# One delta-rule decoder layer: GpSimd in the order of emission, six buffers for queries and P, four for A^, two for x, block-join copies on ScalarE

## The chip, the cores and the metric

The kernel runs as one launch on one core of one Trainium2 chip. A core has five engines that each work through a queue of their own: TensorE (PE) for matmuls and transposes, VectorE (DVE), ScalarE (ACT), GpSimd (POOL), and SyncE (SP), which here only issues DMAs. [...] The metric is device microseconds (us) of one execution; lower is better.

## The reference

A decoder layer on x of shape (4, 512, 512), float32 throughout, with three residual parts. The change lies in the first, a gated delta rule with 16 heads of 128:

```python
x = x + attn(layernorm(x))        # delta rule, below
x = x + cross_attn(layernorm(x), ctx)   # 16 heads of 32, quantised
x = ffn(layernorm(x))             # causal attention with RoPE, then 8 experts, 2 per token; both residuals inside

# attn, per batch and head
q, k, v = (silu(causal_conv4(x @ W.T)) for W in (Wq, Wk, Wv))
g = exp(-exp(A_log) * softplus(x @ Wa.T + dt_bias)); beta = sigmoid(x @ Wb.T)
q, k = q / norm(q), k / norm(k)
for t in range(512):              # the state S is 128 x 128
    error = v[t] - g[t] * (S.T @ k[t])
    S = g[t] * S + outer(k[t], beta[t] * error)
    o[t] = S.T @ q[t]
o = o * rsqrt(mean(o * o) + 1e-6) * norm_w * silu(x @ Wg.T)
return o @ Wo.T
```

## The kernel before, in words

The recurrence is done in chunks of 128 tokens. Inside a chunk, the effect of the tokens on each other is a triangular system whose matrix (called A^ here, tile `at`) is inverted; between chunks a 128x128 state is carried. The work is cut into 32 *pairs* m = 0 to 31: 4 batches times 8 pairs of heads (HG = 2). A pair goes through these generators:

- `stage1(m)`: keys. Projection and convolution (`conv`, whose matmuls are L503, and its three DVE products L514), transposes with sums of squares `ss` (L551, L557), five small GpSimd operations on [128, 8] tiles L558 to L562 (`rk` is a power, `ee` and `ke` scales, `nr` norms), the decay matrix `em` (a scan on DVE L567, then scaled on ACT L397 by `ee`), `at` (L579) which goes to DRAM and comes back as 32x32 blocks `iA` (L633). Then queries: `qg` (query times decay, GpSimd L590), P = keys times queries times decay (`pt`, DVE L601), and the query norm `rq`, which goes through a DMA from `sr` (L614) and two GpSimd operations (L622, L623).
- `stage2_inverse(m)`: elimination of the 32x32 diagonal blocks in 31 steps of two operations, L644 and L645 (`iW`, `iT`), on DVE for even m and on GpSimd for odd m; then a transposed copy (L649) on the same engine. The results go to DRAM (L648, L650) and come back as the 128x128 tiles `T` (L653) and `X` (L655).
- `stage2_values(m)`: values `vn` and gates `gs`.
- `stage3(m)`: the *join* of the inverted blocks into a 128x128 inverse, by small matmuls (L704 and L705, L714 and L716, L727, L736) with copies out of PSUM in between (`Y`, L707 and L708; `T` and `X`, L718 to L720), then the chain over four chunks (L758, L760, L767, L769, L777, L782) with output products L785 and L787, and a tail: `og` (L796), `cv` (L800), its square on ACT (L804), added into `acc` on GpSimd (L805). `rb` is the row of query norms (L742); the gate product `gs * rb` is L745 on GpSimd.
- `output(m)`: output projection (L825), summed in `xa`; after the last pair of a batch, the norm and the residual.
- `prologue(b)`: layernorm, transposes and gates of the next batch, with x loaded at L406. `prepare()` computes keys and values of the cross attention ahead of the loop.

The main loop takes stage3 of pair m, and between its steps it advances, by `turns`, output of m-1 by one step, stage1 of m+2 by two, values of m+1 by one and the inverse of m+1 by two:

```python
            rest = turns(*rest)
            for _ in stage3(m):
                next(rest, None)
            run(rest)
```

`stage3` yields 15 times, so 30 of the 31 elimination steps are emitted inside this loop, and the 31st after stage3's tail. The emission order is only a priority: a planner reorders each engine's queue by its own estimate of when inputs are ready. On TensorE it keeps almost to the emission; on DVE and GpSimd it moves much. [...] Tiles are in pools: a tile named with bufs=4 has four places, and the fifth waits until the first one's readers are done. After the 32 pairs come cross attention, causal attention and experts, which the change doesn't touch.

Of the kernel before, what the change touches and what calls it, by code (L numbers as in the profile page):

```python
# [98 lines left out]
def decoder(ctx: ExitStack, tc: tile.TileContext, a: dict, out: bass.AP):  # L99
# [69 lines left out]
    def idle(n):  # L169
        for _ in range(n):  # L170
            yield
# [154 lines left out]
    with ExitStack() as st:  # L326
# [74 lines left out]
        def prologue(b):  # L401

            x = []
            for c in range(TB):
                t = w2.tile([P, D], F32, name="x_in", bufs=4)
                nc.sync.dma_start(t, x_t[:, b * TB + c, :])  # L406
                x.append(t)
            yield
            yield
            for c, t in enumerate(x):  # L410
                run(layernorm(t.unsqueeze(1), t.unsqueeze(1), small))
                if c == 0:
                    xnT = s2.tile([P, KD, S], F32, name="xnT", bufs=2)
                    seqs[b] = [xnT]
                tp = p_b.tile([P, KD, P], F32, name="pb")
                for kd in range(KD):
                    nc.tensor.transpose(tp[:, kd, :], t[:, kd * P : (kd + 1) * P], ident)
                nc.scalar.copy(xnT[:, :, c * P : (c + 1) * P], tp)
                yield
            pab = p_b.tile([P, TB, 32], F32, name="pb")  # L420
            for c in range(TB):
                for kd in range(KD):
                    nc.tensor.matmul(pab[:, c, :], xnT[:, kd, c * P : (c + 1) * P], wab[:, kd, :], start=kd == 0, stop=kd == KD - 1)
            g_a, lg, beta, gam, ngam, gend, gall = (seq.tile([P, H1, TB], F32, name=n) for n in ("g_a", "lg", "beta", "gam", "ngam", "gend", "gall"))
            nc.scalar.activation(beta, pab[:, :, 16:32].rearrange("p i h -> p h i"), AF.Sigmoid)
            nc.vector.tensor_tensor(g_a, pab[:, :, 0:16].rearrange("p i h -> p h i"), along(dtb, TB), ALU.add)


            y, z, w = (small.tile([P, H1, TB], F32, name=n, bufs=1) for n in ("sp_y", "sp_z", "sp_w"))
            nc.vector.scalar_tensor_tensor(y, g_a, -1.0, g_a, ALU.mult, ALU.min)  # L430
            nc.scalar.activation(y, y, AF.Exp)
            yield
            nc.vector.tensor_scalar(w, y, 2.0, None, ALU.add)
            nc.vector.reciprocal(w, w)
            nc.vector.tensor_tensor(z, y, w, ALU.mult)
            nc.vector.tensor_tensor(w, z, z, ALU.mult)
            nc.vector.tensor_scalar(y, w, 1.0 / 17, None, ALU.mult)
            for n in (15, 13, 11, 9, 7, 5, 3):
                nc.vector.scalar_tensor_tensor(y, y, 1.0 / n, w, ALU.add, ALU.mult)
                if n in (11, 5):  # L440
                    yield
            nc.vector.scalar_tensor_tensor(y, y, 1.0, z, ALU.add, ALU.mult)
            nc.vector.tensor_scalar(y, y, 2.0, None, ALU.mult)
            nc.vector.scalar_tensor_tensor(y, g_a, 0.0, y, ALU.max, ALU.add)
            nc.vector.scalar_tensor_tensor(y, y, -1.0, along(alog, TB), ALU.mult, ALU.mult)

            nc.vector.tensor_scalar(lg, y, -200.0, None, ALU.max)
            yield

            lgf = lg.rearrange("p h i -> p (h i)")  # L450
            pg = p_b.tile([P, 3, H1 * TB], F32, name="pb")
            for n, m in enumerate((C_UP, C_LO, C_ONE)):
                nc.tensor.matmul(pg[:, n, :], tab_a[:, m, :], lgf, start=True, stop=True)
            for n, dst in enumerate((gam, gend, gall)):
                nc.scalar.activation(dst.rearrange("p h i -> p (h i)"), pg[:, n, :], AF.Exp)
            nc.vector.tensor_scalar(ngam, gam, -1.0, None, ALU.mult)
            yield

            nc.vector.tensor_scalar(y, lg, -87.0, None, ALU.max)
            nc.vector.tensor_scalar(z, y, float(np.log2(np.e)), None, ALU.mult)  # L460
            nc.vector.tensor_scalar(z, z, MAGIC, MAGIC, ALU.add, ALU.subtract)
            nc.vector.scalar_tensor_tensor(y, z, -0.693145751953125, y, ALU.mult, ALU.add)
            nc.vector.scalar_tensor_tensor(y, z, -1.42860677e-06, y, ALU.mult, ALU.add)
            yield
            nc.vector.tensor_scalar(w, y, 1.0 / 5040, None, ALU.mult)
            for n in (720, 120, 24, 6, 2, 1):
                nc.vector.scalar_tensor_tensor(w, w, 1.0 / n, y, ALU.add, ALU.mult)
            n2 = small.tile([P, H1, TB], mybir.dt.int32, name="n2", bufs=1)
            nc.vector.tensor_scalar(n2, z, 127.0, None, ALU.add)
            nc.vector.tensor_scalar(n2, n2, 23, None, ALU.logical_shift_left)  # L470
            nc.vector.scalar_tensor_tensor(w, w, 1.0, n2.bitcast(F32), ALU.add, ALU.mult)
            yield

            tp = p_b.tile([H1 * TB, 2, P], F32, name="pb")
            nc.tensor.transpose(tp[:, 0, :], w.rearrange("p h i -> p (h i)"), ident)
            nc.tensor.transpose(tp[:, 1, :], gam.rearrange("p h i -> p (h i)"), ident)
            gr = w2.tile([P, TB * 64], F32, name="Y6").rearrange("p (n t) -> p n t", n=2)[0 : H1 * TB]
            nc.scalar.copy(gr, tp)
            nc.gpsimd.memset(gr[:, 0, 0:1], 0.0)
            for n in range(2):  # L480
                nc.sync.dma_start(g_d[b, n], gr[:, n, :])
            seqs[b] += [beta, gam, ngam, gend, gall]
            yield
# [38 lines left out]
        def stage1(m):  # L522
# [48 lines left out]
            for p in range(HG):  # L571
                scale(em[p], em[p], ee, p)
                pk = p_b.tile([P, TB, P], F32, name="pb")
                for c in range(TB):
                    k_ = kT[p][:, c * P : (c + 1) * P]
                    nc.tensor.matmul(pk[:, c, :], k_, k_, start=True, stop=True)
                at = live.tile([P, TB, P], F32, name="at", bufs=6)
                ats.append(at)
                nc.vector.scalar_tensor_tensor(at, pk, -1.0, em[p], ALU.mult, ALU.mult)  # L579
                nc.sync.dma_start(squares(at_d[m % SLOTS][p * TB : (p + 1) * TB]), at)  # L580
# [5 lines left out]
            for p in range(HG):  # L586
                q = s1.tile([P, S], F32, name="qh")
                yield from conv(b, hg, p, 0, wq, q)
                g = live.tile([P, S], F32, name="qg", bufs=4)
                nc.gpsimd.tensor_tensor(g, q, mb[p], ALU.mult)  # L590
                qg.append(g)
                t = w2.tile([P, S], F32, name="cv", bufs=5)
# [4 lines left out]
                for c in range(TB):  # L597
                    cs = slice(c * P, (c + 1) * P)
                    nc.tensor.matmul(pq[:, c, :], kT[p][:, cs], q[:, cs], start=True, stop=True)
                t = live.tile([P, TB, P], F32, name="pt", bufs=4)  # L600
                nc.vector.tensor_tensor(t, pq, em[p], ALU.mult)  # L601
                pt.append(t)
                yield
# [86 lines left out]
        def stage3(m):  # L690
# [13 lines left out]
                    nc.tensor.matmul(py[lo[p], c, :], ats[p][:, c, 32:64], Ts[p][:, c, 0:32], start=True, stop=True)  # L704
                    nc.tensor.matmul(py[hi[p], c, :], ats[p][:, c, 96:128], Ts[p][:, c, 64:96], start=True, stop=True)  # L705
            for p in range(HG):
                nc.vector.tensor_copy(Yd[p][32:64, :, 0:32], py[lo[p]])  # L707
                nc.scalar.copy(Yd[p][96:128, :, 32:64], py[hi[p]])  # L708
            yield
            px = p_b.tile([P, TB, 96], F32, name="pb")  # L710
# [4 lines left out]
                for p in range(HG):  # L715
                    nc.tensor.matmul(px[half[p], c, 0:64], Yd[p][:, c, :], odd(Xs[p][:, c, :]), start=True, stop=True)  # L716
            for p in range(HG):
                nc.vector.tensor_copy(Ts[p][32:64, :, 0:32], px[lo[p], :, 64:96])  # L718
                nc.scalar.copy(Xs[p][0:32, :, 32:64], px[lo[p], :, 0:32])
                nc.vector.tensor_copy(Xs[p][64:96, :, 96:128], px[hi[p], :, 32:64])  # L720
            yield

            Y6 = []
# [17 lines left out]
            t = w2.tile([P, HG, S], F32, name="rrow", bufs=1)  # L741
            nc.sync.dma_start(chunks(t), r_d[m % SLOTS].rearrange("c t -> (c t)").partition_broadcast(P))  # L742
            rb = [t[:, p, :] for p in range(HG)]
            for p in range(HG):
                nc.gpsimd.tensor_tensor(gs[p], gs[p], rb[p], ALU.mult)  # L745

            st_ = [None] * HG
            po = [p_o.tile([P, TB, P], F32, name=f"po{p}") for p in range(HG)]
            for c in range(TB):
# [34 lines left out]
                for p in range(HG):  # L784
                    nc.tensor.matmul(po[p][:, c, :], us[p], pt[p][:, c, :], start=True, stop=c == 0)  # L785
                    if c > 0:
                        nc.tensor.matmul(po[p][:, c, :], st_[p], qg[p][:, cs], start=False, stop=True)  # L787
                st_ = nst
                yield

            og = []
# [18 lines left out]
        def output(m):  # L810
# [4 lines left out]
            wot = w2.tile([P, HG, D], F32, name="wot", bufs=2)  # L815
            nc.sync.dma_start(wot, a["a_wo"][hg])
            xs = []
            if hg == NHG - 1:
                for c in range(TB):
                    xs.append(w2.tile([P, D], F32, name="x_in", bufs=4))  # L820
                    nc.sync.dma_start(xs[c], x_t[:, b * TB + c, :])
            for c in range(TB):
                pw = p_b.tile([P, D], F32, name="pb")
                for p in range(HG):
# [7 lines left out]
            if hg == NHG - 1:  # L832
# [6 lines left out]
                rsqrt(rs, pq, small, add=1e-6, mul=1.0 / VD)  # L839
                yield  # L840
                for c in range(TB):
                    xr = xs[c]
                    nc.vector.scalar_tensor_tensor(xr, xa[c], rs[:, c : c + 1], xr, ALU.mult, ALU.add)

                    (nc.gpsimd if m == NP - 1 else nc.sync).dma_start(x1d[b * TB + c], xr)
                    yield

        def prepare():

            ctx_ = [w2.tile([P, D], F32, name="og", bufs=2) for _ in range(2)]  # L850
            for kt in range(2):
                nc.sync.dma_start(ctx_[kt], a["ctx"][kt * P : (kt + 1) * P])
            wk = [w2.tile([P, D], F32, name="x_in", bufs=4) for _ in range(KD)]
            for kd in range(KD):
                nc.sync.dma_start(wk[kd], a["b_wkv"][kd * P : (kd + 1) * P, 0:D])
            wv = [w2.tile([P, HG, D], F32, name="wot", bufs=2) for _ in range(2)]
# [31 lines left out]
            for c in range(KD):  # L888
# [14 lines left out]
                yield  # L903
                nc.sync.dma_start(x_val_d[:, :, c * P : (c + 1) * P], t.rearrange("p (k c) -> p k c", k=2))

        NP = B * NHG
        load_weights(0, 1, 0, 2, 3, by=nc.scalar)
        start = prologue(0)
# [11 lines left out]
        for m in range(NP):  # L920
# [13 lines left out]
                wx = top.enter_context(tc.tile_pool(name="b_x", bufs=2, side="right", reuse_waits="tile"))  # L934
                rest.append((cross(0), 2))
            if m:
                rest.append((output(m - 1), 1))
            if m + 2 < NP:
                if (m + 2) % NHG == 0:
                    assert (m + 2) // NHG in seqs  # L940
# [574 lines left out]
```

## Time and profile before

The median of three runs is 3922.55 us (3909.57 to 3927.0). The profiled execution took 3921.34 us, its span is 3919.6 us.

| What | us |
|---|---|
| span of the profiled execution | 3919.6 |
| start of the join of pair 0 (first L704) | 148.5 |
| start of the join of pair 31 | 2113.1 |
| PE busy over the span | 3487.2 |
| DVE busy | 2238.4 |
| ACT busy | 1522.5 |
| POOL busy | 1373.3 |
| PE busy between 148.5 and 2113.1 (1964.6 long) | 1766.48 |
| DVE busy there | 1270.76 |
| ACT busy there | 787.81 |
| POOL busy there | 924.44 |
| mean granted TensorE clock, whole span | 0.941 of full |

Times are those of one execution, read by the hardware profiler. "Busy" leaves out instructions that only wait, branch or issue a DMA. A wait is written as *waiting instruction <- what released it*, with the total, the count and the longest. A line number is a line of the kernel before. "T0" below is the start of the first join matmul (L704) of a pair, and "T0+30" is 30 us later.

### The profile page before, as it was taken

To read this page: it belongs to the slowest core of one execution; us is meant where nothing else is said; L and a number is where in the kernel's file an instruction comes from. 1 tells how busy PE (TensorE), PEld (TensorE's weight loads), DVE (VectorE), ACT (ScalarE), POOL (GpSimd) and SP (SyncE) were. 2 spreads that over 40 slices of the span, in tenths; PEclk is the share of its full clock that TensorE was granted. 3 is DMA by queue.
4 is the path that set the end of the run, shared out by engine and by line. 5 is a ranking of instruction groups with operands and counts; after the bars stand their busy time and mean duration, and the time that the engine had idled before them with its cause. 6 is when DMAs were issued, how large, how long until landed. Compare 5 with 4: busy or idle time off the path is not lost. (4 is left out here: it accounts for less than half of the span.)

```text
span 3919.6 us, 48951 instructions
## 1 busy us (share of the span) xinstructions
PE 3487.2 (89%) x16466; PEld 1984.1 (51%) x16466; DVE 2238.4 (57%) x5115; ACT 1522.5 (39%) x4190; POOL 1373.3 (35%) x1941
## 2 busy tenths in 40 slices
PE   5898899898989989898989799998998999897897
PEld 3455555555555555555555445554554555453343
DVE  5576657675766666756765466555665655543111
ACT  3434443334343434334333244443443444433121
POOL 1443554344435552455335222112212211210442
PEclk8899999899999998999999899998999999898898
DMA  5324332433243333343332444445444444445344
GB/s 163 107 77 123 98 103 80 130 101 111 82 119 119 98 100 106 97 119 104 96 98 87 158 145 154 137 132 132 146 127 137 153 146 139 141 152 183 79 82 93
DMA packets 391881, 465.56 MB, mean 119 GB/s; under 512 B 128451, under 2 KB 242115, under 8 KB 391440
## 3 DMA queue, kind: packets, MB, share of 16 engines
q1 hardware_dynamic: 380080, 438.03, 37.1%
q0 software_dynamic: 10112, 21.58, 3.1%
q8 instruction: 132, 2.16, 0.2%
q10 hardware_dynamic: 1440, 2.84, 0.2%
q14 instruction: 117, 0.96, 0.1%
HBM read 401.76 MB, written 64.81 MB: 119 GB/s over the span
## 5 line engine op out<-in xcount | busy, mean ns | idle before, releaser
L503 PE MATMUL pb<-xnT,w 128*128 128x512 f32 x2048 | 954.9, 605 | 0.0
L503 PEld LDWEIGHTS pb<-xnT,w 128*128 128x128 f32 x2048 | 381.9, 195 | 423.7 <-issue 419.7
L514 DVE SCALAR_TENSOR_TENSOR cv<-pb,pp,cv 128x511 f32<-128x511 f32 (+2 forms) x576 | 427.3, 742 | 153.0 <-ACT cv L511 144.2
L1067 PE MATMUL pb<-c_q,hT 128*128 128x512 f32 x768 | 362.9, 609 | 7.9 <-DMA c_q<-in_c_wq_dram 3.6
L644 POOL TENSOR_TENSOR iW<-iA,iT 32x31 f32<-32x31 f32 (+15 forms) x496 | 249.3, 503 | 210.3 <-DMA iA<-at_d 140.5
L825 PE MATMUL pb<-wot,og 128*128 128x512 f32 x512 | 264.9, 642 | 32.8 <-DVE og L796 26.5
L645 POOL TENSOR_TENSOR iT<-iT,iW 32x31 f32<-32x31 f32 (+15 forms) x496 | 275.1, 555 | 39.0
L1173 PE MATMUL pw<-c_o,oT 128*128 128x512 f32 x512 | 244.8, 611 | 21.9 <-DMA c_o<-in_c_wo_dram 15.5
L511 ACT ACTIVATE cv<-pb,pp 128x512 f32<-128x512 f32 x192 | 148.2, 772 | 261.2 <-PE pb L503 260.7
L1067 PEld LDWEIGHTS pb<-c_q,hT 128*128 128x128 f32 x768 | 143.8, 196 | 162.2 <-issue 149.4
L1139 ACT ACTIVATE e<-pb,nm,rq 128x128 f32<-128x128 f32 (+3 forms) x256 | 158.0, 626 | 104.2 <-DVE nm L1137 75.2
L274 POOL TENSOR_SCALAR x_e<-x_e 128x1024 f32<-128x1024 f32 x64 | 68.7, 1073 | 334.0 <-ACT x_e L269 256.6
L644 DVE TENSOR_TENSOR iW<-iA,iT 32x31 f32<-32x31 f32 (+15 forms) x496 | 178.4, 360 | 11.7 <-DMA iA<-at_d 0.2
L645 DVE TENSOR_TENSOR iT<-iT,iW 32x31 f32<-32x31 f32 (+15 forms) x496 | 177.4, 358 | 11.9
L269 ACT ACTIVATE x_e<-pb,nm 128x256 f32<-128x256 f32 x256 | 118.1, 475 | 164.2 <-DVE nm L266 160.7
L1163 PE MATMUL po<-eT,val 128*128 128x512 f32 x320 | 171.6, 630 | 10.0 <-ACT eT L1161 7.7
L1133 PE MATMUL pb<-kT,qT 128*128 128x256 f32 (+3 forms) x576 | 163.5, 410 | 3.6 <-ACT x_e L269 3.6
L558 POOL TENSOR_TENSOR rk<-ss,mhalf 128x8 f32<-128x8 f32 x32 | 53.1, 1659 | 322.0 <-DVE ss L557 321.9
L579 DVE SCALAR_TENSOR_TENSOR at<-pb,em 128x512 f32<-128x512 f32 x64 | 44.3, 692 | 199.9 <-ACT em L397 199.9
L1173 PEld LDWEIGHTS pw<-c_o,oT 128*128 128x128 f32 x512 | 94.4, 194 | 125.5 <-issue 92.1
L1420 PE MATMUL pb<-w_gu,eT 128*128 x312 | 142.7, 601 | 3.8 <-issue 3.8
L825 PEld LDWEIGHTS pb<-wot,og 128*128 128x128 f32 x512 | 89.7, 194 | 110.3 <-issue 53.3
(324 smaller groups left out, 6609.7 us busy)
## 6 DMA issues: line engine op xcount, KB each, us to landing
c_o<-in_c_wo_dram SPq DMA_DIRECT2D x128, 512.0 KB, 4.1
c_q<-in_c_wq_dram SPq DMA_DIRECT2D x128, 512.0 KB, 4.6
w<-in_a_w_dram SPq DMA_DIRECT2D x124, 512.0 KB, 3.7
row<-g_d SPq DMA_DIRECT2D x64, 512.0 KB, 3.8
at_d<-at SPq DMA_DIRECT2D x64, 256.0 KB, 4.2
T<-t_d SPq DMA_DIRECT2D x32, 512.0 KB, 6.1
X<-x_d SPq DMA_DIRECT2D x32, 512.0 KB, 6.1
rrow<-r_d SPq DMA_DIRECT2D x32, 512.0 KB, 4.7
```

The lines of the kernel that those rows point to most:

```text
L503: nc.tensor.matmul(pj, wt[:, kd, p * P : (p + 1) * P], xnT[:, kd, :], start=kd == 0, stop=kd == KD - 1)
L511: nc.scalar.activation(ac, pj, AF.Identity, bias=cb[:, m, h : h + 1], scale=cw[:, m, h, 3:4])
L514: nc.vector.scalar_tensor_tensor(ac[:, j:], pj[:, : S - j], cw[:, m, h, 3 - j : 4 - j], ac[:, j:], ALU.mult, ALU.add)
L644: eng.tensor_tensor(u, A[:, i, i + 1 :].unsqueeze(2).to_broadcast([nb, n, w]), T[:, i, :w].unsqueeze(1).to_broadcast([nb, n, w]), ALU.mult)
L645: eng.tensor_tensor(T[:, i + 1 :, :w], T[:, i + 1 :, :w], u, ALU.add)
L825: nc.tensor.matmul(pw, og[p][:, c * P : (c + 1) * P], wot[:, p, :], start=p == 0, stop=p == HG - 1)
L1067: nc.tensor.matmul(pj, hT[:, kd, :], w[:, kd % 2, :], start=kd == 0, stop=kd == KD - 1)
L1133: nc.tensor.matmul(ps[:, m, k * P : (k + w) * P], qT[g][:, n + m, :], kT[:, g, j : j + w, :], start=True, stop=True)
L1139: nc.scalar.activation(e[n + m][:, :nk], ps[:, m, :nk], AF.Exp, bias=nm[:, n + m : n + m + 1], scale=rq, accum_out=es[:, n + m : n + m + 1])
L1163: nc.tensor.matmul(po, val[:, g, :], eT, start=k == 0, stop=k == c)
L1173: nc.tensor.matmul(pw, oT[:, h + m, :], w[:, m, :], start=g == 0 and h + m == 0, stop=g == 3 and h + m == 3)
L1420: nc.tensor.matmul(pg, hT[:, kd, :], w_gu[:, bass.ds(e, 1), kd, :, :], start=kd == 0, stop=kd == KD - 1)
```

## The change

1. GpSimd's queue is taken out of the planner's hands (`manual_schedule`): from the first weight loads to the end of the delta rule it issues in the order of emission.
2. Buffers: `qg` 4 to 6, `pt` 4 to 6, `at` 6 to 4, `x_in` 4 to 2.
3. x with two places: `prologue` of batches 1 to 3 loads chunks 0 and 1 ahead and chunk c+2 after the transposes of chunk c; batch 0 puts two of its chunks into `xa` places. `output` of a batch's last pair likewise, and its sum is written into `xa` instead of `x_in`. `prepare` keeps four weight tiles in `qg` and `pt` places.
4. The six join copies that were on DVE (L707, L718, L720, two heads each) go to ACT.
5. The two gate products (L745) are emitted one by one after chunks 1 and 2 of the chain, not before it.
6. `output(m-1)` starts one turn later (`idle(1)`).

```diff
         def prologue(b):
             x = []
-            for c in range(TB):
-                t = w2.tile([P, D], F32, name="x_in", bufs=4)
+
+            def load(c):
+
+                t = w2.tile([P, D], F32, name="xa", bufs=4) if b == 0 and c > 1 else w2.tile([P, D], F32, name="x_in", bufs=2)
                 nc.sync.dma_start(t, x_t[:, b * TB + c, :])
                 x.append(t)
+            for c in range(TB if b == 0 else 2):
+                load(c)
...
                 nc.scalar.copy(xnT[:, :, c * P : (c + 1) * P], tp)
+                if b > 0 and c + 2 < TB:
+                    load(c + 2)
...
-                at = live.tile([P, TB, P], F32, name="at", bufs=6)
+                at = live.tile([P, TB, P], F32, name="at", bufs=4)
...
-                g = live.tile([P, S], F32, name="qg", bufs=4)
+                g = live.tile([P, S], F32, name="qg", bufs=6)
...
-                t = live.tile([P, TB, P], F32, name="pt", bufs=4)
+                t = live.tile([P, TB, P], F32, name="pt", bufs=6)
...
-                nc.vector.tensor_copy(Yd[p][32:64, :, 0:32], py[lo[p]])
+                nc.scalar.copy(Yd[p][32:64, :, 0:32], py[lo[p]])
...
-                nc.vector.tensor_copy(Ts[p][32:64, :, 0:32], px[lo[p], :, 64:96])
+                nc.scalar.copy(Ts[p][32:64, :, 0:32], px[lo[p], :, 64:96])
...
-                nc.vector.tensor_copy(Xs[p][64:96, :, 96:128], px[hi[p], :, 32:64])
+                nc.scalar.copy(Xs[p][64:96, :, 96:128], px[hi[p], :, 32:64])
...
-            for p in range(HG):
-                nc.gpsimd.tensor_tensor(gs[p], gs[p], rb[p], ALU.mult)
...
                 st_ = nst
+                if 0 < c <= HG:
+                    nc.gpsimd.tensor_tensor(gs[c - 1], gs[c - 1], rb[c - 1], ALU.mult)
                 yield
...
             if hg == NHG - 1:
-                for c in range(TB):
-                    xs.append(w2.tile([P, D], F32, name="x_in", bufs=4))
-                    nc.sync.dma_start(xs[c], x_t[:, b * TB + c, :])
+                load(0)
+                load(1)
...
-                    xr = xs[c]
-                    nc.vector.scalar_tensor_tensor(xr, xa[c], rs[:, c : c + 1], xr, ALU.mult, ALU.add)
+                    xr = xa[c]
+                    nc.vector.scalar_tensor_tensor(xr, xr, rs[:, c : c + 1], xs[c], ALU.mult, ALU.add)
+                    if c + 2 < TB:
+                        load(c + 2)
...
-            wk = [w2.tile([P, D], F32, name="x_in", bufs=4) for _ in range(KD)]
+            wk = [live.tile([P, S], F32, name="qg", bufs=6) for _ in range(2)]
+            wk += [chunks(live.tile([P, TB, P], F32, name="pt", bufs=6)) for _ in range(2)]
...
+        st.enter_context(tc.manual_schedule(engines={mybir.EngineType.Pool}))
         NP = B * NHG
...
-                rest.append((output(m - 1), 1))
+                rest.append((chain(idle(1), output(m - 1)), 1))
```

More of the change, by code (lines that the diff above doesn't have):

```diff
@@ L403, in prologue @@
             x = []
-            for c in range(TB):
-                t = w2.tile([P, D], F32, name="x_in", bufs=4)
+            def load(c):
+                t = w2.tile([P, D], F32, name="xa", bufs=4) if b == 0 and c > 1 else w2.tile([P, D], F32, name="x_in", bufs=2)
                 nc.sync.dma_start(t, x_t[:, b * TB + c, :])
                 x.append(t)
+            for c in range(TB if b == 0 else 2):
+                load(c)
             yield
             yield
-            for c, t in enumerate(x):
+            for c in range(TB):
+                t = x[c]
                 run(layernorm(t.unsqueeze(1), t.unsqueeze(1), small))
@@ L817, in output, with load @@
             xs = []
+            def load(c):
+                xs.append(w2.tile([P, D], F32, name="x_in", bufs=2))
+                nc.sync.dma_start(xs[c], x_t[:, b * TB + c, :])
             if hg == NHG - 1:
-                for c in range(TB):
-                    xs.append(w2.tile([P, D], F32, name="x_in", bufs=4))
-                    nc.sync.dma_start(xs[c], x_t[:, b * TB + c, :])
+                load(0)
+                load(1)
             for c in range(TB):
```

## The prediction, written before the result was known

> **What bounds the kernel now.** I read the busy table first, then the stretches of two neighbouring pairs (18, whose partner inverse 19 is on GpSimd, and 19), then the waits, then the timeline around the handover from one pair to the next. In the stretches the columns are length, then PE, PEld, DVE, ACT and POOL busy, PE clock.
>
> ```profile
> PE 3487.2 (89%) x16466; PEld 1984.1 (51%) x16466; DVE 2238.4 (57%) x5115; ACT 1522.5 (39%) x4190; POOL 1373.3 (35%) x1941
> ...
> 1309.60:1371.50 61.90, 55.81 (x297) 32.55 (x296) 41.52 (x86) 24.79 (x71) 31.36 (x46) 0.97 0.36 102
> 1371.50:1432.90 61.40, 55.70 (x301) 31.82 (x303) 41.62 (x82) 24.95 (x71) 25.04 (x40) 0.97 0.35 104
> ```
>
> PE bounds each pair: some 56 of 62 us. Between 148.5 and 2113.1 it idles 1964.6 - 1766.5 = 198 us, which is all that better cover could return, the clock apart. The waits:
>
> ```profile
> POOL rk L558 <- DVE ss L557: 321.9, 17, 25.3
> POOL rq L622 <- DMA rq<-sr: 247.2, 12, 28.7
> ACT em L397 <- POOL ee L560: 166.2, 32, 11.1
> DVE pt L601 <- PE po L785: 94.2, 24, 6.2
> PE ps L777 <- ACT u L769: 45.0, 13, 6.0
> PE pb L727 <- DVE cv L514: 22.2, 14, 2.3
> ```
>
> The third and fifth are one story. In even pairs the planner puts `rk` behind the odd inverse; by the timeline of pair 16 (T0 = 1182.5) `ss` ended at T0+27.9 and `rk` began at T0+33.5; ACT waited in `em` with the `u` copies behind it, and PE for `u`:
>
> ```profile
> 1216.01 1.65 POOL L558 TENSOR_TENSOR rk<-ss,mhalf 128x8 f32<-128x8 f32 x1
> ...
> 1218.30 2.45 ACT L397 ACTIVATE em<-em,ee 128x128 f32<-128x128 f32 x8 [8.54 <-POOL ee L560]
> ...
> 1221.61 0.90 PE L777 MATMUL ps<-u,kdec 128*128 128x128 f32 x4 [4.64 <-ACT u L769]
> ...
> 1222.00:1232.00 10.00, 9.24 (x42) 8.65 (x42) 7.21 (x15) 4.27 (x10) 1.01 (x1) 0.50 0.48 145
> ```
>
> The last line shows the aftermath: clock 0.50 for 10 us. Ten even pairs with such a late `rk` last 64.6 to 66.9 us; pairs 10 and 18, where it is 1 to 3 us late, 61.7 and 61.9.
>
> The handover 18 to 19:
>
> ```profile
> 1335.40 0.24 POOL L645 TENSOR_TENSOR iT<-iT,iW 32x31 f32<-32x31 f32 x1
> ...
> 1370.21 0.30 POOL L622 TENSOR_SCALAR rq<-rq 128x8 f32<-128x8 f32 x1 [27.47 <-DMA rq<-sr]
> 1370.60 1.79 POOL L623 TENSOR_TENSOR rq<-rq,mhalf 128x8 f32<-128x8 f32 x1
> ...
> 1374.89 3.53 POOL L805 TENSOR_TENSOR acc<-acc,cv 128x512 f32<-128x512 f32 x2
> ...
> 1371.19 0.39 PE L787 MATMUL po<-qg,state 128*128 128x128 f32 x2
> 1371.51 0.22 PE L704 MATMUL pb<-T,at 128*32 128x32 f32 x1
> ```
>
> Inverse 19's last step ended at 1335.6, `T` landed at 1345.3, and the join that reads it came at 1371.5: over odd pairs `T` is 26 to 40 us early. GpSimd adds `acc` of pair 18 only after that join has begun.
>
> [...]
>
> **The change, part by part.** I compared the built orders of both programs, queue by queue.
>
> *GpSimd's order.* In every even pair m the queue is now: both `acc` of m-1; steps 1 to 10 of inverse m+1; `rk` to `nr` of m+2; steps 11 to 16; gs, qg; steps 17 to 22; gs, qg; steps 23 to 26; both `rq`; steps 27 to 30; both `acc` **of m**; step 31; the copy. Before, the `acc` ahead of the copy were those of m-1, since the planner ran the odd inverse half a pair earlier. In PE's order the join of m+1 directly follows the last L787 of m in all 31 handovers. So `T` of an odd pair can't leave before stage3(m) has ended, and PE has nothing to do meanwhile. Worked out from the last L787's end (E = 1371.6):
>
> GpSimd path: sr to `rq` landed at 1370.2, E-1.4. Both `rq` 2.1, steps 27 to 30 (L644 and L645 from 32x135 to 32x60 in the timeline) 3.4: E+4.1. `acc` 2 x 1.27 = 2.5, step 31 with gaps 0.6: E+7.2. The other branch, og 2 x 0.74, cv 2 x 0.68, square 0.63, is ready at E+3.5 and hidden. Then the DMAs: the write L648 lands after 2.2 to 2.3, the issue of the read takes 0.2 to 1.2, L653 lands after 3.9 at best, median 6.1: 6.3 to 9.6. Join at E+13.5 to E+16.8; I take 15.2. Is GpSimd free by then? Its sum in between: from T0+6.6 (acc of m-1) ten steps 11.0; wait for `ss` at T0+27.5; key operations 2.5; six steps 8.6; gs and qg 2.5, qg waiting for its query at about T0+44; six steps 8.3; gs, qg, the query at T0+55; four steps 4.5: T0+61, against `rq` at T0+60.6. It just fits; what it slips adds to the hole.
>
> Fifteen handovers (to pairs 1 to 29): 15 x 15.2 = 228. To pair 31: stage3(30) is short (35.6 us), and GpSimd needs T0+6.6, the whole inverse (32.8 busy plus 62 gaps of 0.08 = 37.8), two gs 2.5, `acc` and DMAs 11: T0+58, so 22. Together +250. After each hole PE restarts at half clock: after its 8.6 us gap ending at 186.5 the clock read 0.50 to 194. I take 5.6 us at half, 2.8 lost, x 16 = +45 (bounds 20 and 65).
>
> *What it returns.* `rk` early in ten even pairs: 65.2 - 61.8 = 3.4 each, and the same in 4, 12 and 20: -44. Join copies: 192 leave DVE (192 x 0.285 = 55 us busy) for ACT (192 x 0.257 = 49), hidden by ACT's 60% idle; PE's L727 no longer waits behind L514: -22 of its waits, less if ACT is in its own queue. Output a turn later: PE waited 26.5 for `og` in L825: -18. Six `qg` and `pt`: DVE's 94 us of waits for L785 go, and `pt` no longer stands ahead of `og`; only what PE waits for DVE in L767 and L758 (57 us) can come back: -11. Sum -95; bounds 0 and the 198 of all idling.
>
> *Free edits.* gs after chunks 1 and 2: at T0+40 to 55, hidden by the chain up to `og` at T0+62; without that cover 1.3 each. `at` with four: its readers end in the join of m, written again for m+2; cover 20 us. x with two places: 14 loads move behind transposes or sums, two turns (8 us) ahead, against 3.5 to landing; SP holds weights and A^ behind them, used a pair later; if uncovered, 14 x 3.5 = 49. The four tiles in `qg` and `pt` places are released before pair 2 needs them. The queues after the delta rule are nearly the same; PE's is identical.
>
> Sum: 3919.6 + 250 + 45 - 95 = 4119.6; the profiled run lies 1.7 above its span and 1.2 below the median, so 4121 for the median.
>
> **Rivals.** *Faster:* the holes don't show, because `T` comes in time, and only the returns stay: 3922 - 95 = 3827. It decides where a handover costs under 95/16 = 6 us. For it: the waits on `ee` are real and go. Against: the DMA round trip alone is 6.3, and it starts after `acc` of the same pair. *GpSimd falls behind:* its two-input steps at times take 1.4 instead of 0.6 us (L644 at 1316.03); if waits in its fixed order make it 8 us late at `rq`, holes are 23: +128, 4250. Against: `rk`, qg and `rq` each wait for others, which gives slack back. *Nothing moves:* the planner's order was the emission's anyway, 3922. Against: the `acc` of another pair stands before the copy.
>
> **Numbers.** Holes as worked out 0.82; late GpSimd 0.10; faster 0.05; nothing 0.03. The main case spans 4035 (short DMAs, more returns: 15 x 13.5 + 20 + 25 - 135 = +112) to 4190 (holes 17.5, few returns: 262 + 22 + 55 - 70 = +269). I take 4030 to 4205 as the range. Within 0.5% (20 us) is about what a measurement of this kernel can't tell from no change. Slower 0.93, same 0.03, faster 0.04.
>
> **What would show it.** After: PE idle 13 to 17 us before the first L704 of odd pairs, none before even ones, `T` as releaser; `acc` of the same pair just before step 31; `rk` at once after `ss`, PE's 4.6 us gap at T0+34 gone, even pairs up to that hole 60 to 62 us; DVE no longer waiting in `pt`. I am wrong if `T` lands before the last L787, if even pairs don't shrink, or if ACT's copies delay the joins.

## The result, and the profile after

The changed kernel takes 4113.2 us (median of four, 4105.0 to 4125.7), beside 3918.4 for the kernel before: 1.0493 times as long, 95% interval 1.046 to 1.0525. Predicted were 4121. The profiled execution took 4110.9 us, its span is 4109.1.

The busy row, and the stretches of pair 18 up to its last product, the gap after it, and pair 19 (columns as before the change: length, PE, PEld, DVE, ACT and POOL busy, clock):

```profile
PE 3469.9 (84%) x16466; PEld 1952.2 (48%) x16466; DVE 2325.8 (57%) x4923; ACT 1568.8 (38%) x4382; POOL 1382.5 (34%) x1941
...
1401.30:1463.90 62.60, 54.99 (x297) 31.84 (x296) 43.95 (x74) 26.29 (x77) 43.05 (x67) 0.95 0.26 77
1463.90:1479.60 15.70, 0.05 (x1) 0.00 (x0) 14.94 (x28) 1.82 (x3) 9.80 (x14) 0.67 0.49 135
1479.60:1535.60 56.00, 54.77 (x296) 31.45 (x296) 29.78 (x53) 24.42 (x74) 7.42 (x9) 0.97 0.36 103
```

Between the two pairs lie 15.7 us in which PE does nothing. The second surprise is in the third line: pair 19 has lost 12 us of VectorE work (41.6 before) and is 5.4 us shorter. The waits of the whole span (lines 566, 652 and 653, 712, 766 and 773 are the former 558, 644 and 645, 704, 760 and 767):

```profile
POOL rk L566 <- DVE ss L565: 615.2, 32, 33.4
PE pb L712 <- DMA T<-t_d: 212.3, 14, 19.1
...
PE ps L773 <- DVE r L766: 107.0, 46, 8.0
...
ACT em L397 <- POOL ee L568: 72.1, 32, 3.1
```

PE now waits for `T`, and, more than before, for `r` from VectorE. The line of before:

```profile
PE ps L767 <- DVE r L760: 36.8, 41, 1.5
```

ScalarE's longest wait in `em` is 3.1 us instead of 11.1. The handover from 18 to 19, line by line (GpSimd, then the DMA queue, then PE):

```profile
1463.46 1.78 POOL L631 TENSOR_TENSOR rq<-rq,mhalf 128x8 f32<-128x8 f32 x1
1465.32 0.41 POOL L652 TENSOR_TENSOR iW<-iA,iT 32x135 f32<-32x135 f32 x1
...
1469.07 2.73 POOL L813 TENSOR_TENSOR acc<-acc,cv 128x512 f32<-128x512 f32 x2
1471.88 0.29 POOL L652 TENSOR_TENSOR iW<-iA,iT 32x31 f32<-32x31 f32 x1
1472.24 0.37 POOL L653 TENSOR_TENSOR iT<-iT,iW 32x31 f32<-32x31 f32 x1
...
1472.64 0.32 SPq L656 DMA_DIRECT2D t_d<-iT  x1
1475.10 0.56 SPq L661 DMA_DIRECT2D T<-t_d  x1
...
1463.56 0.39 PE L793 MATMUL po<-qg,state 128*128 128x128 f32 x2
1479.60 0.26 PE L712 MATMUL pb<-T,at 128*32 128x32 f32 x1 [15.65 <-DMA T<-t_d]
```

Counted from E = 1463.9, the end of pair 18's last output product: `rq` until E+1.3, steps 27 to 30 until E+5.1, both `acc` until E+7.9, step 31 until E+8.7, the write issued at once, the read 2.5 us later, the join 4.5 us after that.

What the pairs show, in all kernels of this study (read from the one profiled execution of each; mean us of the 15 odd pairs, of the 12 even ones without a layernorm of the next batch, and of the 3 with it, each without the hole at its end; then the mean hole before odd and before even pairs, and the one before pair 31; a hole is PE's idling between a pair's last output product and the next join):

| kernel | median | odd | even | with layernorm | hole, odd | hole, even | hole, 31 |
|---|---|---|---|---|---|---|---|
| before | 3918.4 | 61.9 | 64.4 | 75.8 | 0 | 0 | 0 |
| after | 4113.2 | 56.8 | 63.4 | 83.0 | 14.9 | 0 | 19.1 |
| e1 planner | 3914.0 | 57.9 | 65.3 | 86.4 | 0 | 0 | 0 |
| e2 fixed order alone | 4373.9 | 57.8 | 58.3 | 88.1 | 34.3 | 0 | 23.9 |
| e3 three steps | 3886.7 | 54.9 | 64.5 | 89.9 | 0 | 0 | 15.0 |
| e4 acc later | 4072.6 | 56.6 | 63.5 | 86.9 | 12.2 | 0 | 16.2 |
| e5 copies on VectorE | 3925.2 | 57.0 | 64.4 | 91.1 | 0 | 0 | 14.6 |
| e6 late blocks | 3891.9 | 54.9 | 64.5 | 91.1 | 0 | 0 | 14.9 |
| e7 x in four places | 3902.3 | 55.9 | 64.3 | 89.1 | 0 | 0 | 15.3 |
| e8 both | 3899.5 | 55.9 | 64.4 | 88.9 | 0 | 0 | 15.4 |
| e9 e2 + six `qg` | 4206.1 | 58.3 | 64.1 | 93.8 | 17.1 | 0 | 21.9 |
| e10 all on GpSimd | 3904.5 | 55.3 | 58.9 | 90.3 | 1.8 | 2.7 | 17.5 |
| e11 VectorE fixed too | 4162.1 | 63.1 | 59.5 | 89.0 | 1.2 | 12.6 | 3.4 |
| e12 one set of blocks | 3911.8 | 60.9 | 57.2 | 85.4 | 1.8 | 0 | 26.2 |

The profiled execution of e12 was the slowest of its eleven (3928.1 us), that of e7 the fastest of its five (3893.5), so by their medians these two rows are some 0.5 us a pair too long and 0.3 too short.

From before to after, span to span: +223.4 (15 holes) +18.1 (pair 30, with its hole) -77.0 (odd pairs) -12.4 (even) +21.4 (with layernorm) +1.4 (start) +14.6 (from the join of pair 31 on) = 189.5, by which the spans differ.

### The profile page after: what moved, and what is told of

It reads as the page before. It is cut to its first block, busy times and chain, and to the rows that moved or that the text cites. A ratio compares the mean times of both kernels' runs of the same rounds, so it can differ in the third digit from the quotient of the medians.

```text
span 4109.1 us, 48875 instructions
## 1 busy us (share of the span) xinstructions
PE 3469.9 (84%) x16466; PEld 1952.2 (48%) x16466; DVE 2325.8 (57%) x4923; ACT 1568.8 (38%) x4382; POOL 1382.5 (34%) x1941
## 5 line engine op out<-in xcount | busy, mean ns | idle before, releaser
L511 PE MATMUL pb<-xnT,w 128*128 128x512 f32 x2048 | 987.7, 623 | 0.9 <-DVE xa L842 0.9
L652 POOL TENSOR_TENSOR iW<-iA,iT 32x31 f32<-32x31 f32 (+15 forms) x496 | 265.6, 536 | 38.9
L653 DVE TENSOR_TENSOR iT<-iT,iW 32x31 f32<-32x31 f32 (+15 forms) x496 | 250.3, 505 | 13.1
L837 PE MATMUL pb<-wot,og 128*128 128x512 f32 x512 | 252.3, 616 | 0.0
L652 DVE TENSOR_TENSOR iW<-iA,iT 32x31 f32<-32x31 f32 (+15 forms) x496 | 238.8, 482 | 12.6
L712 PE MATMUL pb<-T,at 128*32 128x32 f32 x512 | 17.6, 221 | 242.4 <-DMA T<-t_d 212.3
L598 POOL TENSOR_TENSOR qg<-qh,row 128x512 f32<-128x512 f32 x64 | 82.5, 1290 | 372.4 <-ACT qh L525 238.6
L1180 PE MATMUL po<-eT,val 128*128 128x512 f32 x320 | 172.3, 632 | 10.6 <-ACT eT L1178 8.4
L773 PE MATMUL ps<-r,X 128*128 128x128 f32 x384 | 80.2, 309 | 107.2 <-DVE r L766 107.0
```

Source lines behind the costliest of these rows:

```text
L511: nc.tensor.matmul(pj, wt[:, kd, p * P : (p + 1) * P], xnT[:, kd, :], start=kd == 0, stop=kd == KD - 1)
L652: eng.tensor_tensor(u, A[:, i, i + 1 :].unsqueeze(2).to_broadcast([nb, n, w]), T[:, i, :w].unsqueeze(1).to_broadcast([nb, n, w]), ALU.mult)
L653: eng.tensor_tensor(T[:, i + 1 :, :w], T[:, i + 1 :, :w], u, ALU.add)
L837: nc.tensor.matmul(pw, og[p][:, c * P : (c + 1) * P], wot[:, p, :], start=p == 0, stop=p == HG - 1)
L1180: nc.tensor.matmul(po, val[:, g, :], eT, start=k == 0, stop=k == c)
```

## The experiments

**e1. All of the change but the fixed order.**

```diff
-        st.enter_context(tc.manual_schedule(engines={mybir.EngineType.Pool}))
```

> The changed kernel, but GpSimd's queue is left to the planner again; buffers, copies on ScalarE, later gate products and the turn of delay stay. Theory (the loss is the fixed order alone, since the tail of pair m stands before the 31st step of the odd inverse): the holes before the joins of odd pairs go, so 223 + 18 us of idling and most of some 45 us of half clock come back, and `rk` is late again in even pairs (+30): 4113 - 241 - 20 + 30, about 3880, between 3830 and 3930. Rival (the other parts cost: copies on ScalarE delay the joins, x with two places stalls the prologue): holes stay or others come, above 4030.

Measured 3914.0 us, 0.9984 times the kernel before (0.9975 to 0.9993). No hole is left, so the holes need the fixed order. What is left are the effects of the other parts: odd pairs 4 us shorter than before, the three with a layernorm 10.6 us longer. There PE stands 19 to 20 us, as in pair 20 (timeline, then the waits):

```profile
1468.78 1.11 PE L423 MATMUL pb<-tab,x_in 128*128 128x128 f32 x4 [19.95 <-DVE xa L842]
...
DVE ln_st L131 <- DMA x_in<-in_x_dram: 67.3, 6, 20.4
```

VectorE waits up to 20.4 us for the third chunk of x and PE for its transposes: with two places its load comes late. In the kernel before that wait was 4.5 us in all. The prediction had counted this edit as free (49 us if uncovered).

**e2. The fixed order alone, in the kernel before.**

```diff
+        st.enter_context(tc.manual_schedule(engines={mybir.EngineType.Pool}))
```

> The kernel before with GpSimd in the order of emission and nothing else. Theory: holes of 13 to 17 us before the 15 joins of odd pairs and a longer one before pair 31, as in the changed kernel; no help from the other parts, though `rk` comes early: 4090 to 4160. Rival (the other parts cost): below 3990, with holes under 5 us.

Measured 4373.9 us, 1.1159 (1.1128 to 1.119): slower than the theory allowed by 210 us. The holes are 34 us long. The handover 16 to 17 (GpSimd, then PE; line numbers of the kernel before):

```profile
1469.83 1.26 POOL L590 TENSOR_TENSOR qg<-qh,row 128x512 f32<-128x512 f32 x1 [19.27 <-PE po L785]
1471.17 0.62 POOL L644 TENSOR_TENSOR iW<-iA,iT 32x255 f32<-32x255 f32 x1
...
1469.66 0.39 PE L787 MATMUL po<-qg,state 128*128 128x128 f32 x2
1504.74 0.23 PE L704 MATMUL pb<-T,at 128*32 128x32 f32 x1 [34.69 <-DMA T<-t_d]
```

With four places, `qg` of pair m+2 can't be written until pair m's last output products have read theirs. In a fixed order GpSimd stands there for 19 us with 15 steps of the inverse behind it, all of which PE then waits for.

**e3. Three steps a turn for the inverse on GpSimd.** The changed kernel with

```diff
-                rest.append((stage2_inverse(m + 1), 2))
+                rest.append((stage2_inverse(m + 1), 3 if m % 2 == 0 else 2))
```

> The changed kernel, but an inverse on GpSimd is advanced by three steps a turn instead of two, so all 31 steps, the copy and the DMAs are emitted by turn 13, ahead of the tail of stage3. Theory: `T` lands before the last output product of pair m, all 16 holes go, and `rk` still comes early, since only 15 steps stand before it: 4113 - 241 - 25 to -45, that is 3820 to 3860. Rival A (GpSimd is too slow whatever the order, so that it only gets to the end of the inverse after the pair's end): holes of 8 us or more stay, above 3980. Rival B (the holes are not what costs; PE waits for something else then): above 4050.

Measured 3886.7 us, 0.9919 (0.9888 to 0.995): 226 less than the changed kernel, and the fastest of this study. Fifteen of the sixteen holes are gone (the expectation said all: in the short pair 30, 34.6 us long, GpSimd works on the inverse from T0+5.7 to T0+43.1, and 15 us stay). The same handover, and the wait that is left:

```profile
1324.44 0.32 SPq L656 DMA_DIRECT2D t_d<-iT  x1
1326.99 0.38 SPq L661 DMA_DIRECT2D T<-t_d  x1
...
1337.84 0.22 PE L712 MATMUL pb<-T,at 128*32 128x32 f32 x1
...
PE ps L773 <- DVE r L766: 119.5, 46, 11.5
```

`T` is asked for 10.9 us ahead of the join. That settles the hole, pair 30 apart: it is a matter of where the last steps stand in the order, not of how much GpSimd has to do. The total is 27 us above the band of the theory. Even pairs, at 64.5 us, have gained nothing against the kernel before, and the three with a layernorm are 14 us longer.

**e4. The additions into `acc` after the inverse.** The changed kernel; the pairs of operands are kept in a list and added after `run(rest)`:

```diff
-                    nc.gpsimd.tensor_tensor(acc[b], acc[b], sq, ALU.add)
+                    later.append((acc[b], sq))
...
             run(rest)
+            add_later()
```

> The changed kernel, but the additions into `acc` are emitted after the 31st step and the copy. Theory, by the terms of the prediction's sum: the hole loses the two additions, 2.5 to 2.7 us, and little else, since `rq` and steps 27 to 30 still stand there: holes of 12 to 12.5 us instead of 14.9, the total 16 x 2.6 = 42 us less, 4060 to 4085. Rival (the tail as a whole is what holds the inverse, and without it the inverse is done at E): holes of 8 us, 4000.

Measured 4072.6 us (1.0385, 1.0355 to 1.0416), inside the 4060 to 4085 of the theory. The hole shrinks from 14.9 to 12.2 us, by the 2.7 us of the two additions. So this term of the hole's sum holds, and `acc` is less than a fifth of the hole; the other terms were not taken out one by one.

**e5. The join copies back on VectorE**, in the kernel of e3:

```diff
-                nc.scalar.copy(Yd[p][32:64, :, 0:32], py[lo[p]])
+                nc.vector.tensor_copy(Yd[p][32:64, :, 0:32], py[lo[p]])
```

and the same for the copies of `T` and of the upper `X`.

> The kernel with three steps a turn (3886.7), but the six join copies are back on VectorE. Theory (the copies' move is worth something, since PE's joins no longer wait behind convolution products and elimination steps on VectorE): pairs 1 to 2 us longer, 30 to 60 in all, 3915 to 3950. Rival (the odd pairs' gain of 4 to 7 us has other causes, ScalarE's queue is no shorter): 3870 to 3900.

Measured 3925.2 us, 1.0 (0.999 to 1.0009): 38 us more than e3 by the medians, 32 by the ratios, as much as the theory said, and nearly all of it in odd pairs (57.0 against 54.9 us, x 15 = 32). The path is not the theory's: in e5's odd pairs no join waits for a convolution product or a step on VectorE. PE idles 2.5 us in one instead of 1.4, 0.6 of it for `kT` and 0.3 for `r`, at a mean clock of 0.988 instead of 1.000. Why the copies do that stays open.

**e6, e7, e8. Two attempts at the rest.** e6 reads the blocks of an even pair when its inverse begins, e7 gives x four places with its old loads and `pt` four, e8 does both, all in the kernel of e3:

```diff
-            load_blocks(m, ats)
+            if m % 2 == 0 and m > 0:
+                inverses[m] = ats
+            else:
+                load_blocks(m, ats)
...
-                t = live.tile([P, TB, P], F32, name="pt", bufs=6)
+                t = live.tile([P, TB, P], F32, name="pt", bufs=4)
```

> The kernel with three steps a turn (3886.7), but the blocks `iA` of an even pair are read from DRAM only when its inverse begins, so that VectorE eliminates in the odd pair, where GpSimd has no elimination. Theory (two engines eliminating at the same time slow VectorE's steps from 0.34 to 0.70 us, and `r` stands behind them): VectorE's elimination falls from 438 us to 350 or less, the wait of L773 for `r` from 120 to under 50 us, even pairs from 64.5 to about 60.5; odd pairs grow by at most 2 us: 3886.7 - 48 - 10 + 20, about 3850, between 3825 and 3875. Rival (the order of VectorE's queue alone is what delays `r`, wherever the steps run): the wait only moves to odd pairs, which grow by 4 us or more: 3885 to 3930.

> The kernel with three steps a turn (3886.7), with x in four places and loaded as in the kernel before, and P (`pt`) in four for it. Theory (two places for x stall the three pairs with a prologue: PE waits up to 5 us each for transposes of the layernorm): those pairs fall from 89.9 to some 78, -36, pair 31 and the start 3 less; `pt` with four places costs under 10: about 3850, between 3835 and 3865. Rival (six places for `pt` are needed under the fixed order: VectorE stands in `pt` with `r` behind it): even pairs 2 to 4 us longer, 3880 to 3910.

> Both edits of the two runs before together. Theory: the gains add, 3886.7 - 37 - 37, about 3813, between 3790 and 3845; faster than the kernel before by some 2.5%. Rival (the second edit's gain is the same idling of PE): no better than the better one of the two, 3850.

Measured 3891.9 (0.9905, 0.9879 to 0.9932), 3902.3 (0.9933, 0.9911 to 0.9954) and 3899.5 us (0.9927, 0.9901 to 0.9953): no gain anywhere. In e6 nothing moved. The line in the program is later, but the planner orders VectorE and the DMA queue itself and started the even inverse where it had; VectorE's elimination took 440 us, in e3 438. e6 therefore tested nothing. In e7 the pairs with a layernorm stay at 89 us, so the theory failed; the total lies in the rival's band, but even pairs, which the rival had 2 to 4 us longer, stay at 64.3. The pairs with a layernorm have another wait (waits of e7):

```profile
DVE x_in L137 <- POOL ln_rs L123: 57.9, 12, 8.5
```

`ln_rs`, a GpSimd power like `rk`, stands in the fixed order behind steps of the odd inverse, and VectorE and PE wait for it. By these waits, two places for x cost about 10 us a batch under the planner (e1, where other parts were changed too), while under the fixed order `ln_rs` is late anyway and x hides behind it. This reading is argued; no run moved `ln_rs`. Odd pairs are 1 us longer in e7; that `pt` with four places does this is likely, and wasn't tried alone.

**e9. The fixed order and six `qg`**, in the kernel before: e2 with

```diff
-                g = live.tile([P, S], F32, name="qg", bufs=4)
+                g = live.tile([P, S], F32, name="qg", bufs=6)
```

and `at` in four places to pay for it.

> The kernel before with GpSimd in the order of emission (4373.9) and one thing more: six places for `qg`, paid for by four for `at`. Theory (with four places the `qg` of pair m+2 waits for the last output product of pair m, and in a fixed order 14 or so steps of the odd inverse stand behind it; six places let it pass): the hole falls from 34 us to the 15 of the changed kernel, 4374 - 15 x 19 = 4090, with copies still on VectorE between 4080 and 4150. Rival (P with four places, or the copies on VectorE, make the longer hole): holes stay above 28 us, 4280 to 4380.

Measured 4206.1 us (1.0721, 1.0688 to 1.0754), 168 less than e2. The hole falls from 34.3 to 17.1 us: the theory's direction, and most of its size. The 15 holes give back 258 us, but the total only 168 and ends 56 us above the expected band, because even pairs grow from 58.3 to 64.1 us (12 x 5.8 = 70) and those with a layernorm by 5.7. In e2 GpSimd stood still while VectorE eliminated in the even pair; in e9 it no longer does: VectorE's elimination takes 502 us instead of 421, and PE's wait for `r` (L767) doubles, from 49.2 to 95.3 us. The next section takes up what that means.

**What slows the even pairs.** In the changed kernel the last `r` of pair 18 comes 6.4 us late (VectorE, GpSimd, then PE):

```profile
1448.28 0.60 DVE L652 TENSOR_TENSOR iW<-iA,iT 32x156 f32<-32x156 f32 x1
1448.92 0.66 DVE L653 TENSOR_TENSOR iT<-iT,iW 32x156 f32<-32x156 f32 x1
...
1455.01 0.33 DVE L766 SCALAR_TENSOR_TENSOR r<-ps,ngam,vn 128x128 f32<-128x128 f32 x1
...
1448.13 0.58 POOL L652 TENSOR_TENSOR iW<-iA,iT 32x231 f32<-32x231 f32 x1
1448.79 0.62 POOL L653 TENSOR_TENSOR iT<-iT,iW 32x231 f32<-32x231 f32 x1
...
1455.39 0.79 PE L773 MATMUL ps<-r,X 128*128 128x128 f32 x2 [6.43 <-DVE r L766]
```

`r` stands behind steps of the inverse for pair 20, and these run in the rhythm of GpSimd's steps for pair 19. The groups, of the kernel before and then of the changed one (busy, mean ns of one):

```profile
L644 DVE TENSOR_TENSOR iW<-iA,iT 32x31 f32<-32x31 f32 (+15 forms) x496 | 178.4, 360 | 11.7 <-DMA iA<-at_d 0.2
L645 DVE TENSOR_TENSOR iT<-iT,iW 32x31 f32<-32x31 f32 (+15 forms) x496 | 177.4, 358 | 11.9
```

```profile
L653 DVE TENSOR_TENSOR iT<-iT,iW 32x31 f32<-32x31 f32 (+15 forms) x496 | 250.3, 505 | 13.1
...
L652 DVE TENSOR_TENSOR iW<-iA,iT 32x31 f32<-32x31 f32 (+15 forms) x496 | 238.8, 482 | 12.6
```

The same 992 instructions take 489 us instead of 356. Sorted by whether GpSimd is busy meanwhile, and compared only at the same places of the elimination, one takes 338 ns alone and 700 ns where GpSimd is busy for four fifths of it or more (41 places; 332 and 623 ns at 45 places if half is enough). Before, 101 of 992 ran beside GpSimd for half of their time or more, now 509: 321 of these beside an elimination step (532 ns, 341 alone at the same 31 places), 176 beside other work of GpSimd (786 and 340 ns).

Ahead of the late `r` stand 18 of these instructions, from T0+38.6 on, and VectorE is never idle meanwhile. Together they take 5.7 us longer than instructions of their shapes do alone, and PE waits 6.4 us; seven other even pairs show the same two numbers within 0.1. So in these pairs the slowed steps are most of the wait. Three runs took the coincidence away.

**e10. All inverses but the first on GpSimd**, three steps a turn, in the kernel of e3:

```diff
-            eng = nc.vector if m % 2 == 0 else nc.gpsimd
+            eng = nc.vector if m == 0 else nc.gpsimd
```

> The kernel with three steps a turn (3886.7), all inverses but the first on GpSimd, three steps a turn for each. Theory (VectorE's elimination beside GpSimd's is what delays `r` in even pairs): VectorE loses some 420 us of work, the wait of L773 for `r` falls from 120 to under 40 us, even pairs from 64.5 to 57 or 58; odd pairs 55 to 57: about 3805, between 3775 and 3845. Rival (GpSimd, with 33 us of elimination and 10 of other work in every pair of 55 us and its own waits in the fixed order, gets to the end of the inverse too late): holes of 5 us or more before even pairs, above 3890.

Measured 3904.5 us, 0.9957 (0.9942 to 0.9971).

```profile
PE pb L712 <- DMA T<-t_d: 85.3, 25, 17.5
...
PE ps L773 <- DVE r L766: 24.2, 36, 1.5
```

Theory and rival are both half right. The wait for `r` falls from 119.5 to 24.2 us and even pairs from 64.5 to 58.9 (61.2 with the hole), as the theory said. But GpSimd is then busy from T0+4 to T0+57 of pair 18 with one gap of 0.8 us, and `T` is late in 25 of the 31 handovers, mostly by some 3 us.

**e11. VectorE in the order of emission too**, in the kernel of e3:

```diff
-        st.enter_context(tc.manual_schedule(engines={mybir.EngineType.Pool}))
+        st.enter_context(tc.manual_schedule(engines={mybir.EngineType.Pool, mybir.EngineType.DVE}))
```

> The kernel with three steps a turn (3886.7), and VectorE too in the order of emission, so that it eliminates for the even pair inside the odd pair. Theory (the two eliminations at once are what costs in even pairs): both stand apart, VectorE's steps fall from 0.44 to about 0.34 us, 438 to 340 us in all; the wait for `r` in even pairs falls below 50 us; 3820 to 3870. Rival (in a fixed order VectorE stands in `at` or in a convolution product with the chain's `r` behind it, as GpSimd stood): waits for `r` grow in all pairs, above 3930.

Measured 4162.1 us (1.0605, 1.0575 to 1.0635). VectorE's elimination falls to 357 us and even pairs to 59.5, as the theory said. The wait for `r`, by which the rival had the loss, also falls, to 17 us. Most of the loss is the hole of this case over again, on the other engine: at two steps a turn the 31st step on VectorE is emitted after the tail, and 12.6 us of idling stand before every even pair (x 15 = 189). But the rival has a part in it: odd pairs grow from 54.9 to 63.1 us (x 15 = 123), and PE waits in each 3.1 us for `qh`, which ScalarE makes from VectorE's convolution products, and 2.9 us for the state, which VectorE writes; in e3 it waits for neither. Three steps a turn on VectorE too was not tried. The waits of the whole span:

```profile
PE pb L712 <- DMA T<-t_d: 211.1, 24, 13.1
...
PE pb L607 <- ACT qh L525: 106.4, 51, 11.6
...
PE ps L764 <- DVE state L788: 43.0, 15, 3.0
...
PE ps L773 <- DVE r L766: 17.1, 20, 3.3
```

**e12. One set of the elimination's tiles**, so that the two inverses can't run at once; three steps a turn for all, in the changed kernel:

```diff
-            A, T, W = (t[m % 2 * nb : (m % 2 + 1) * nb] for t in elim)
+            A, T, W = (t[0:nb] for t in elim)
```

with the blocks of every pair after the first read when its inverse begins.

> The changed kernel with three steps a turn for every inverse, and one set of the elimination's tiles (`iA`, `iT`, `iW`) in place of two, the blocks read when the inverse begins. So VectorE's elimination for an even pair can't begin before GpSimd's for the odd pair has left the tiles; in the built order of VectorE its steps now stand among the `r` of the odd pair, where with two sets 22 of 31 stood before the odd pair's first `r`. Theory (both engines eliminating at once is what costs in even pairs): VectorE's elimination falls from 438 to about 340 us, the wait for `r` from 120 to under 40 us, even pairs from 64.5 to 58 to 60, odd pairs grow from 54.9 to 56 to 58: about 3840, between 3800 and 3875. Rival (the steps in front of `r` cost the same wherever they stand, or one set makes `T` late in a new place): the idling moves to odd pairs or into holes of 3 us and more, 3880 or above.

Measured 3911.8 us, 0.9964 (0.9953 to 0.9975); the groups, and the wait for `r`:

```profile
L657 DVE TENSOR_TENSOR iW<-iA,iT 32x31 f32<-32x31 f32 (+15 forms) x496 | 176.7, 356 | 9.6
L658 DVE TENSOR_TENSOR iT<-iT,iW 32x31 f32<-32x31 f32 (+15 forms) x496 | 176.4, 356 | 8.0
...
PE ps L778 <- DVE r L771: 48.2, 31, 3.0
```

In e3 nine steps of an even inverse stand ahead of the last `r` of the pair before and the other 22 behind it, all of them before the odd pair's first `r`; now all stand among the odd pair's. The theory's numbers for even pairs come: elimination 353 us, even pairs 57.2 and a hole of 2.3. The rival's come too: odd pairs grow by 6 us, to 60.9, since VectorE now does its elimination there. PE waits in an odd pair 2.4 us for `r` and 1.2 each for the state and `qh`, where in e3 it waits 0.6 for `r` and for neither of the others. An even and an odd pair together are 120.4 us long, against 119.4 in e3. As no step is left in the even pairs, e12 does not part slowed steps from steps as such; the 5.7 of 6.4 us above do. It shows that steps at full speed also cost, where they stand among an odd pair's chain. And pair 31's hole is 26 us: GpSimd starts its last inverse at T0+17.2 of pair 30, in e3 at T0+5.7.

## Why the prediction was right, and where it was not

**What bounds it, and the hole: right.** `acc` of pair m stood before step 31, PE had nothing in between, `T` was the releaser. 14.9 us measured on average (15.7 in pair 18), 15.2 taken. In pair 18 two errors nearly cancel: the queue was 1.5 us later than worked out (step 31 ended at E+8.7, not E+7.2, each term being 0.2 to 0.6 us longer), the DMAs 1.0 faster (7.0 us from the write to the join, against the 8.0 in the middle of 6.3 to 9.6). Before pair 31 it was 19.1, not 22. Sum 242 against 250.

**The clock: mis-sized.** Odd pairs run at 0.959 of the clock after a hole and 56.8 us, in e3 without one at 1.000 and 54.9: 1.9 us a hole, about +30, not +45, if all of this difference is the clock's. That PE restarts at half clock held in all 16 cases: from the first join matmul after the hole the clock read 0.50 for 3.1 to 6.1 us before pairs 1 to 29, on average 4.7, and for 7.3 before pair 31. The 5.6 us were the author's estimate; the one gap named with it gives 7.5 (186.5 to 194).

**The returns: the sum near, its parts wrong.** 189.5 - 242 - 30 leaves -83, against -95. The prediction put 44 of it into even pairs and those with a layernorm, by `rk` (it counted ten even pairs with a late `rk` at 64.6 to 66.9 us; the trace has nine). `rk` did come at T0+25.3, at once after `ss`, and ScalarE's stall in `em` went. But even pairs lost only 1 us, to 63.4, not the 60 to 62 foretold, and those with a layernorm grew by 7.2. What failed is the step that took a freed stall for a gain. Of PE's idling in an even pair (mean of the eleven after pair 0) the waits for `u` (4.0 us) and `og` (1.0) went, but the wait for `r` grew from 1.2 to 7.3. The fixed order had moved the odd elimination later: the inverse for pair 19 ran from T0-19.1 to T0+26.0 of pair 18 before, and runs from T0+5.6 to T0+71.3 now, while VectorE's for pair 20 begins at T0+38.6 instead of T0+46.2. So the two run at once.

Odd pairs gave 5.1 us each instead, with the clock's loss in them: PE idles 1.2 us in one, before it was 5.6, in several small waits. The copies may be some 2.1 of the 5.1 (measured in e5 at three steps a turn). VectorE, busy for 14.9 of the hole's 15.7 us, works off elimination that pair 19 is then spared, but e3's odd pairs follow no hole and are shorter still, so they don't gain by that.

That the total came within 8 us is in part luck: holes 8 and clock 15 us smaller than foretold, returns 12 smaller, these by a gain in odd pairs that was not foretold, in place of one in even pairs that was. The last step of the sum is a slip, too: 4119.6 + 1.7 + 1.2 is 4122.5, not 4121.

**The six buffers: wrong in kind.** They were counted as 11 us of saved waits in `pt`. Under a fixed order six `qg` are what keeps the hole at 15 or 17 us instead of 34 (e2, e9), 168 us in the total. The prediction had both `qg` in GpSimd's queue, and asked when the query would be ready, not when the place would be free.

**The copies: mis-sized.** -22 predicted, -32 by the ratios measured (e5, at three steps a turn), and not by the wait foretold.

**Free edits: not free.** x with two places seems hidden here only because `ln_rs` is later still (e1, e7). In a pair with a layernorm PE now waits 3.4 us for `r`, 3.0 for the normalised x, 2.6 for a convolution product in the join and 2.4 for the state; before, its longest wait there was 5.3, for the transposed x.

**Output a turn later** wasn't tried alone; PE's 26.5 us of waiting for `og` there are gone from the trace.

**After the loop.** Of the 14.6 us after the join of pair 31, 2.7 are in that pair; from there to the end the kernels of this study lie between 1814 and 1829 us, the profile of before at 1806.5, and what sets that is open.

**The rivals.** That GpSimd falls behind didn't happen: it began `rq` 0.8 us before E in pair 18. "Faster" decided at 6 us a handover; e3 is that case made true, at 3887 instead of 3827, the difference being the even pairs, the three with a layernorm (14 us each) and pair 31.

## What to carry to other kernels

Where an engine is taken in the order of emission, ask of each long job whether its last step is emitted before or after the work that ends the stage: here one more step a turn was worth 226 us, and the same fault came back on VectorE in e11. With a fixed order, look for a tile whose write must wait for a place: one blocked write of `qg` held 15 steps of the inverse behind it for 19 us (e2). And a change of order moves work in time: look what that work now runs beside (here VectorE's elimination beside GpSimd: 489 us instead of 356), and what stands behind it.

## What the runs showed that was not expected

Elimination steps on VectorE take 700 instead of 338 ns while GpSimd works; GpSimd's take 528 instead of 480 while VectorE works (changed kernel, 50 places compared). The trace shows when this happens, not by what. In the timeline of pair 18 both engines' steps come every 0.67 us, VectorE's each ending some 0.2 us after GpSimd's. Beside a longer GpSimd operation a VectorE step is longer too, and also ends 0.2 us after it (VectorE beside GpSimd, GpSimd, and the same shape on VectorE in the hole, alone):

```profile
1450.95 1.33 DVE L652 TENSOR_TENSOR iW<-iA,iT 32x192 f32<-32x192 f32 x1
1450.80 1.27 POOL L796 TENSOR_TENSOR gs<-gs,rrow 128x512 f32<-128x512 f32 x1
1477.46 0.35 DVE L652 TENSOR_TENSOR iW<-iA,iT 32x192 f32<-32x192 f32 x1
```

The prediction had no term for this.
